# Message passing over sorted edges: the one-hots of the overflow rows computed ten gathers sooner, their products placed three gathers later, and edge numbers fetched in runs of 512 bytes

## The chip, the cores and the metric

The kernel runs on one core of one Trainium2 chip. The time is that of one execution on the device in microseconds (us); lower is better. Five engines matter: PE (TensorE) multiplies matrices, DVE (VectorE), ACT (ScalarE) and POOL (GpSimd) work on tiles in the on-chip memory, and SP issues direct transfers. Here POOL issues the indirect gathers, one instruction each. Every engine takes its instructions in the order of the program and waits at the first one that isn't ready.

## What is computed

There are N = 6250 nodes with C = 256 values and E = 100000 edges, sorted by destination. After a layer norm and a relu come four rounds of message passing, each followed by three dense layers; the input is added at the end.

```python
def agg(h):
    return jax.ops.segment_sum(h[src], dst, num_segments=N)
for l in range(NL - 1):                       # NL = 4
    h = x + agg(x)
    h = jax.nn.relu(h @ W1s[l] + b1s[l])
    h = jax.nn.relu(h @ W2s[l] + b2s[l])
    x = h @ W3s[l] + b3s[l]
h = x + agg(x)
h = jax.nn.relu(h @ cW1 + cb1)
h = jax.nn.relu(h @ cW2 + cb2)
return h @ cW3 + cb3
...
h = jnp.maximum(_layernorm(x, axis=-1), 0.0)
x = x + _L0_gnn_ref(h, src, dst, ...)
```

## The kernel before

**Nodes, blocks, panels.** The nodes stand in NT = 49 blocks of P = 128. The features, already multiplied by the next W1, lie in `XY`, each value split in a high and a low part. The sum over neighbours is made in two ways.

- *By products.* Eight panels of four blocks (`panels`) have a matrix of edge counts, one byte per entry. `build` makes it once, while layer 0 runs: for two steps of 128 edges it forms one-hots of the edges' ends on DVE (`one_hot`, L1067, tiles `lo` and `hi`, one batch ahead, two buffers each), multiplies them on PE (L1108, tile `bp`, two buffers) and casts the result to bytes (L1116 on ACT, every fourth on DVE at L1118). `product` then runs over the 49 source blocks, one *unit* each: four matmuls of 512 columns (L1566) that read one cast tile `a`. `prepare` asks for those casts (L1539 on ACT, L1541 on DVE) three units ahead in layer 0 and five later.
- *By gathers.* The blocks of `gone` (17, in layer 0 four more) get their neighbours' rows from a table in HBM. A node has K = 17 direct rows; what is beyond that goes to OV = 2 *overflow* gathers of 128 rows for the whole block, which a matmul with a one-hot of the receiving nodes distributes. So a block takes SLOT = 19 gathers (L1391, tiles `rows` and `last`).

**Order.** The program is written out unit by unit. `tick` counts units (`now`), and `later(n, f)` runs f n ticks on. `clock` adds up a planner's estimate of the PE time issued so far. The class `Gathered` spreads a layer's gathers evenly over that clock (`begin`, `pace`), and its `events` say after which gather of a block something is done: `pair` adds two tiles of rows into `acc` (L1417, L1419); `fold`, after gather 17, makes u from `XY`, `acc` and the last row (L1429 to L1437) and then the one-hot `hot` (L1439); `add`, after gather 19, multiplies the overflow rows by `hot` on PE (L1445, tile `sums`, two matmuls of which each shows as two in the profile). `finish` adds `sums` to u (L1455) and, some ticks on, transposes u on PE (L1466) and hands it to the dense layers (`mlp`, L1260 and L1289). Other bursts of matmuls are put where `meets` is true, which is when an `add` is due. In the last eight ticks of a layer all its events are due.

**Before the first unit.** `look` finds the edges' place by node, `normed` normalises and multiplies by W1. At its end `look` asks for the first K edges of every node of the 21 gathered blocks: 21 gathers of 17 numbers per partition from `src` straight into `idx` (L820, issued at L607 by `ask`). Then come PRE = 36 ticks that only build, two steps each. At the 25th, `slot_rows` turns `idx` into row numbers with two DVE instructions over all 21 blocks (L852, L853), and layer 0's gathers begin (READY = 50 steps). `overflow` computes the places of a block's overflow edges (L858 to L871) and three ticks later fetches their sources, one number per partition, two gathers, straight into `over`. It is called for the first two blocks at the 23rd and 24th tick, and for each next one while the gathers of the second block ahead of it run.

Of the kernel before, what the change touches and what calls it, by code (L numbers as in the profile page):

```python
# [8 lines left out]
F32 = mybir.dt.float32  # L9
I32 = mybir.dt.int32  # L10
# [4 lines left out]
OP = mybir.AluOpType  # L15
PSUM = bass.MemoryType.PSUM
DRAM = bass.MemoryType.DRAM
P = 128
# [378 lines left out]
def sorted_edges(  # L397
# [38 lines left out]
    nc = tc.nc  # L436
    N, C = x.shape
# [16 lines left out]
    K, OV = 17, 2  # L454
    SLOT = K + OV
# [14 lines left out]
    NG = sum(n for _, n in gone)  # L470
# [17 lines left out]
    nodes3 = const.tile([P, 3, NG], F32, name="nodes3")  # L488
    gained = const.tile([P, NG], F32, name="gained")
    from_i = over[:, 0, :]  # L490
    taken = const.tile([P, NG, 2], BF16, name="taken")
    slots = const.tile([P, OV * P], BF16, name="slots")
    kth = const.tile([P, K], F32, name="kth")
    line = const.tile([P, OV], F32, name="line")
    pad = const.tile([P, 2], F32, name="pad")
# [115 lines left out]
            after(got, "edges are asked for a few at a time")  # L611

    def look(pool):
        firsts_i = pool.tile([1, EB], I32, name="near_i", bufs=1)
        with nc.allow_non_contiguous_dma(reason="each tile's first destination"):
            nc.sync.dma_start(out=firsts_i, in_=bass.AP(tensor=dst.tensor, offset=dst.offset,
# [230 lines left out]
        yield  # L847


    def slot_rows():  # L850

        nc.vector.scalar_tensor_tensor(live, idx, pad[:, 1:2], live, op0=OP.add, op1=OP.mult)  # L852
        nc.vector.tensor_scalar(idx, live, pad[:, 0:1], None, op0=OP.add)  # L853

    def overflow(hots, c):

        hit = hots.tile([P, OV * P], BF16, name="hit", bufs=2)
        nc.vector.tensor_scalar(hit, slots, gained[:, c:c + 1], None, op0=OP.is_ge)  # L858
        ps = ps_g.tile([P, W], F32, name="pt")
        for j in range(OV):  # L860
            nc.tensor.matmul(ps[:, 2 * j:2 * j + 2], hit[:, j * P:(j + 1) * P], taken[:, c, :],
                             start=True, stop=True)
        v = ps[:, :2 * OV].rearrange("p (j t) -> p j t", t=2)
        e = hots.tile([P, OV], F32, name="e_f", bufs=2)
        e_i = hots.tile([P, OV], I32, name="e_i", bufs=2)

        def edges():
            nc.vector.tensor_copy(rel[:, c, :], v[:, :, 0])
            nc.vector.scalar_tensor_tensor(e, v[:, :, 1], nodes3[:, 2, c:c + 1], line, op0=OP.add,
                                           op1=OP.add)  # L870
            nc.vector.tensor_scalar(e_i, e, float(E - 1), None, op0=OP.min)  # L871
# [125 lines left out]
    with tc.manual_schedule():  # L997
# [160 lines left out]
        def later(n, fn):  # L1158
            due.append((now[0] + n, fn))
# [181 lines left out]
        class Gathered:  # L1341
            def __init__(self, l):
                self.l, self.sent, self.done = l, 0, 0
                self.first, self.turn = None, None
                self.blocks = [(b, n, i, left[q] + i)
                               for q, (b, n) in enumerate(gone) for i in range(n)
                               if l == 0 or (b, n) != panels[-1]]
                self.alone = {b + i for b, n, i, _ in self.blocks}
                self.rows, self.us, self.acc, self.hot = {}, [], None, None
                self.order = [(g, k) for g in range(len(self.blocks)) for k in range(SLOT)]  # L1350
                self.events = []
                for g in range(len(self.blocks)):
                    for k in range(3, K - 1, 2):
                        self.events.append((SLOT * g + k, lambda g=g, k=k: self.pair(g, k)))
                    self.events.append((SLOT * g + K - 1, lambda g=g: self.fold(g)))
                    self.events.append((SLOT * g + SLOT - 1, lambda g=g: self.add(g)))
                self.n = len(self.events)

            def due(self, early=0.0):
# [5 lines left out]
                        self.first + self.events[self.done][0] * self.pace - early))  # L1365

            def meets(self):
                return self.due() and self.events[self.done][0] % SLOT == SLOT - 1

            def begin(self):  # L1370
                self.first = clock[0] + LEADS[self.l]
# [28 lines left out]
            def advance(self):  # L1400

                if self.first is None:
                    return
                while ahead:
                    overflow(hots, ahead.pop(0))
                self.flow()
                while self.due():
                    at, run = self.events[self.done]
# [12 lines left out]
            def fold(self, g):  # L1421
                if self.turn in jobs:
                    jobs.remove(self.turn)
                    self.turn[2]()
                b, n, i, c = self.blocks[g]
                b += i
                u = work.tile([P, C], F32, name="u", bufs=2)
                self.us.append(u)
                nc.vector.tensor_tensor(u, XY[:, b, :C].bitcast(F32), XY[:, b, C:].bitcast(F32),  # L1429
                                        OP.add)  # L1430
                used.add((self.l, b, 0))
                if (self.l, b, 1) in used:
# [3 lines left out]
                nc.vector.tensor_tensor(u, u, self.acc[:, 1, :], OP.add)  # L1436
                nc.vector.tensor_tensor(u, u, self.rows.pop((g, K - 1)), OP.add)  # L1437
                self.hot = work.tile([P, OV, P], F32, name="hot", bufs=2)
                nc.vector.tensor_tensor(self.hot, colf[:, None, :].to_broadcast([P, OV, P]),  # L1439
                                        rel[:, c, :, None].to_broadcast([P, OV, P]), OP.is_equal)  # L1440

            def add(self, g):
                b, n, i, _ = self.blocks[g]
                for j in range(OV):
                    mm = nc.tensor.matmul(sums[:, :C], self.hot[:, j, :], self.rows.pop((g, K + j)),  # L1445
                                          start=(j == 0), stop=(j == OV - 1))
                    passed(C * FULL32, mm)
                self.finish(b, n, i, sums)
# [253 lines left out]
```

## Time and profile before

| what | value |
|---|---|
| median of 3 runs | 2399.58 us (2398.6 to 2402.63) |
| the profiled execution | 2401.84 us, of which its span is 2400.0 us |
| busy share of the span | PE 88%, PE weight loads 66%, POOL 63%, DVE 52%, ACT 40% |
| first unit of layer 0 | at about 186 us; layers 0 to 3 end at about 858, 1374, 1882 and 2400 us |
| DMA | 375.68 MB, mean 157 GB/s |

A row of the groups view reads: line, engine, operation, what it writes and reads, shape, count | busy us in total, mean ns of one | idle time of the engine just before these instructions, and what ended most of it. A row of the timeline: start and length in us, engine, line, operation, tiles, how many merged, and in brackets the idle time before the first and what ended it. A row of the windows view: the window, its length, busy us and instruction count of PE, PE weight loads, DVE, ACT and POOL, then the granted PE clock, the DMA share and GB/s.

### The profile page before, as it was taken

The numbers are of one execution on the slowest core, as the hardware profiler recorded it, in microseconds if no ns is written. First come the engines' busy times: TensorE is split into PE (matmuls) and PEld (weight loads), VectorE is DVE, ScalarE is ACT, GpSimd is POOL, SyncE is SP. The second block draws the span as 40 slices with busy tenths as digits, with TensorE's granted clock in tenths as the row PEclk, the third lists the DMA queues.
The fourth block names the chain that finished last, engine by engine and source line by source line (L and its number), as shares of the span: only waits on it lengthen the run. The fifth ranks groups of instructions, "written<-read, shape, count | busy, mean of one in ns | idle before, by whom it ended". The sixth has DMA issues, their size and how long they took to land.

```text
span 2400.0 us, 28926 instructions
## 1 busy us (share of the span) xinstructions
PE 2107.7 (88%) x9071; PEld 1578.9 (66%) x9071; DVE 1242.1 (52%) x2785; ACT 962.7 (40%) x1925; POOL 1515.7 (63%) x1495
## 2 busy tenths in 40 slices
PE   5858788787888899999999899989998998999898
PEld 3635565555555577777777777767776776676665
DVE  6867665655566634444344544443445444544444
ACT  4756555555455643233223342322323422232222
POOL 3346677666776627776677357776777276777773
PEclk9958999898999999999999999999999999999999
DMA  5425545544454645445455465454546454555553
GB/s 174 133 85 161 167 149 163 163 149 143 147 168 152 210 146 169 145 140 169 138 163 164 151 191 153 138 168 136 171 138 194 150 180 141 175 161 181 162 180 94
DMA packets 198743, 375.68 MB, mean 157 GB/s; under 512 B 34210, under 2 KB 125474, under 8 KB 198580
## 3 DMA queue, kind: packets, MB, share of 16 engines
q0 software_dynamic: 69024, 182.29, 25.8%
q1 hardware_dynamic: 127630, 189.61, 24.4%
q10 hardware_dynamic: 1926, 1.85, 0.3%
q8 instruction: 73, 1.20, 0.2%
q14 instruction: 90, 0.74, 0.1%
HBM read 313.88 MB, written 59.39 MB: 156 GB/s over the span
## 4 chain that ended last, share of the span: by engine, by line
PE 80%; issue 7%; DVE 5%; ACT 3%; another core or an unknown queue 3%; DMA 1%; POOL 0%; ACTq 0%; DVEq 0%; POOLq 0%
PE agg L1566 57%; PE ps L1260 6%; PE ps L1289 5%; PE bp L1108 4%; PE sums L1445 3%; ACT at L1116 1%; PE ps L1286 1%; ACT a L1539 1%; PE bp L953 1%; PE ps L1466 1%; DVE acc L1419 1%; PE ps L582 1%; DVE hi L1067 0%; DVE lo L1067 0%
## 5 line engine op out<-in xcount | busy, mean ns | idle before, releaser
L1566 PE MATMUL agg<-a,XY 128*128 128x512 f32 x6076 | 1584.7, 413 | 58.1 <-issue 34.9
L1391 POOL DMA_INDIRECT rows<-table,idx x1152 | 1179.3, 1024 | 631.0 <-PE agg L1566 245.2
L1566 PEld LDWEIGHTS agg<-a,XY 128*128 128x128 f32 x6076 | 1157.2, 195 | 340.4 <-issue 68.8
L1539 ACT CAST a<-at 128x512 fp32r<-128x512 uint8 x943 | 565.0, 623 | 797.8 <-PE agg L1566 574.2
L1541 DVE CAST a<-at 128x512 fp32r<-128x512 uint8 x576 | 257.1, 452 | 534.7 <-PE agg L1566 368.9
L1116 ACT CAST at<-bp 128x392 uint8<-128x392 f32 x402 | 184.2, 488 | 296.7 <-PE bp L1108 107.3
L1419 DVE TENSOR_TENSOR acc<-acc,rows 128x512 f32<-128x512 f32 x432 | 295.6, 684 | 2.7 <-DMA rows<-table,idx 0.4
L1108 PE MATMUL bp<-hi,lo 128*128 128x196 bf16 x1024 | 158.1, 272 | 119.1 <-issue 68.7
L1108 PEld LDWEIGHTS <-lo 128*128 128x128 bf16 x1024 | 87.3, 104 | 207.6 <-issue 154.8
L1391 POOL DMA_INDIRECT last<-table,over x144 | 154.2, 1071 | 67.4 <-PE agg L1566 27.8
L1260 PE MATMUL ps<-h,w 128*128 128x512 f32 (+2 forms) x364 | 159.3, 578 | 7.0 <-issue 7.0
L1067 DVE TENSOR_TENSOR lo<-lanes,pairs 128x512 bf16<-128x512 bf16 x256 | 107.2, 419 | 73.1 <-remote 32.1
L1067 DVE TENSOR_TENSOR hi<-cols,pairs 128x784 bf16<-128x784 bf16 x256 | 142.8, 558 | 0.0
L1289 PE MATMUL ps<-w,h 128*128 128x256 f32 x588 | 135.9, 383 | 3.5 <-ACT h L1473 1.8
L1289 PEld LDWEIGHTS ps<-w,h 128*128 128x128 f32 x588 | 112.5, 192 | 21.8 <-ACT h L1473 2.6
L1118 DVE CAST at<-bp 128x392 uint8<-128x392 f32 x110 | 62.0, 564 | 121.9 <-PE bp L1108 53.2
L1260 PEld LDWEIGHTS ps<-h,w 128*128 128x128 f32 (+1 forms) x364 | 64.8, 186 | 75.2 <-issue 69.3
L1307 DVE TENSOR_TENSOR zz<-ps,w 128x512 f32<-128x512 f32 (+1 forms) x75 | 49.8, 677 | 122.7 <-PE ps L1289 55.9
L1445 PE MATMUL sums<-last,hot 128*128 128x256 f32 x288 | 81.5, 407 | 35.7 <-DVE hot L1439 20.7
L1455 DVE TENSOR_TENSOR u<-u,sums 128x256 f32<-128x256 f32 x72 | 30.0, 417 | 139.9 <-PE agg L1566 112.7
L1445 PEld LDWEIGHTS sums<-last,hot 128*128 128x128 f32 x288 | 54.9, 198 | 63.3 <-DVE hot L1439 25.3
L1391 POOL DMA_INDIRECT last<-table,idx x72 | 75.0, 1041 | 33.5 <-issue 13.7
(167 smaller groups left out, 1080.8 us busy)
## 6 DMA issues: line engine op xcount, KB each, us to landing
at<-mat SPq DMA_DIRECT2D x214, 448.0 KB
mat<-at SPq DMA_DIRECT2D x32, 784.0 KB
rows<-table,idx POOLq DMA_INDIRECT x1152
table<-zz SPq DMA_DIRECT2D x72, 256.0 KB
back<-table SPq DMA_DIRECT2D x120, 128.0 KB
xs<-in_x_dram SPq DMA_DIRECT2D x8, 768.0 KB
table<-zs SPq DMA_DIRECT2D x24, 256.0 KB
out_dram<-zz SPq DMA_DIRECT2D x24, 256.0 KB
```

The lines of the kernel that those rows point to most:

```text
L1067: nc.vector.tensor_tensor(o.rearrange("p q (n t) -> p q n t", t=2), values.rearrange("p (n t) -> p n t", t=2)[:, None, :, :].to_broadcast( ...
L1108: mm = nc.tensor.matmul(bp[:, m * HW:(m + 1) * HW], lo[:, q + m, :], hi[:, q + m, :], start=True, stop=True)
L1116: nc.scalar.copy(o, v)
L1118: nc.vector.tensor_copy(o, v)
L1260: mm = nc.tensor.matmul(ps[:mp, :w], weights[l][0][:, c, i * P:i * P + mp], h1[:, c, :w], start=(c == 0), stop=(c == KC - 1))
L1289: mm = nc.tensor.matmul(o, h2[0][:, c, nodes], w3[:, c, :], start=(c == 0), stop=(c == KC - 1))
L1391: got = nc.gpsimd.indirect_dma_start(out=t, out_offset=None, in_=tables[self.l][:, :], in_offset=bass.IndirectOffsetOnAxis(ap=at, axis=0),)
L1419: nc.vector.tensor_tensor(self.acc, self.acc, t, OP.add)
L1445: mm = nc.tensor.matmul(sums[:, :C], self.hot[:, j, :], self.rows.pop((g, K + j)), start=(j == 0), stop=(j == OV - 1))
L1539: nc.scalar.copy(o, mat[l, p][j])
L1541: nc.vector.tensor_copy(o, mat[l, p][j])
L1566: mm = nc.tensor.matmul(agg[c][:, :w], XY[:, j, o:o + P], a[:, :w], start=(j == 0 and half == 0), stop=(j == NT - 1 and half == 1))
```

## The change

The one-hot of the overflow rows leaves `fold` and becomes an event of its own (`spots`), due after the ninth gather of its block. `add` is due three gathers later, so it falls among the next block's first gathers, but for a layer's last block. A copy of `src`, padded by 128 numbers, is written to HBM at the very start by two transfers on ACT's queue. The direct edges of a block are then fetched from it 128 numbers (512 bytes) per partition into a scratch tile of the pool `rows`, one block per tick from the first tick on, and turned into row numbers five ticks later by two small DVE instructions per block. The overflow sources are fetched 512 bytes wide too, into two scratch tiles (`run`, two buffers), and their first number is copied out six ticks after the fetch (`keep`), 42 small DVE copies in all. Layer 0's gathers begin two ticks later (READY = 54).

```diff
+    srcs = dram.tile([E + P], I32, name="srcs")
...
     def look(pool):
+        nc.scalar.dma_start(out=srcs[:E].rearrange("(p e) -> p e", p=P - 28),
+                            in_=src.rearrange("(p e) -> p e", p=P - 28))
+        nc.scalar.dma_start(out=srcs[E:].rearrange("(o e) -> o e", o=1),
+                            in_=src[:P].rearrange("(o e) -> o e", o=1))
...
-        nc.vector.tensor_scalar(at0, st, float(E - K), None, op0=OP.min)
+        nc.vector.tensor_scalar(at0, st, float(E), None, op0=OP.min)
         nc.vector.tensor_copy(from_i, at0)
-        for c in range(NG):
-            asks.append((idx[:, c, :], src, from_i[:, c:c + 1]))
-        ask(len(asks))
...
-    def slot_rows():
-        nc.vector.scalar_tensor_tensor(live, idx, pad[:, 1:2], live, op0=OP.add, op1=OP.mult)
-        nc.vector.tensor_scalar(idx, live, pad[:, 0:1], None, op0=OP.add)
+    def slot_rows(gath, c):
+        t = gath.tile([P, 2, C], F32, name="rows", bufs=7)[:, 0, :P].bitcast(I32)
+        asks.append((t, srcs, from_i[:, c:c + 1]))
+        ask(1)
+
+        def turn():
+            w = live[:, c, :]
+            nc.vector.scalar_tensor_tensor(w, t[:, :K], pad[:, 1:2], w, op0=OP.add, op1=OP.mult)
+            nc.vector.tensor_scalar(idx[:, c, :], w, pad[:, 0:1], None, op0=OP.add)
+
+        later(5, turn)
...
         def gather():
+            ts = [hots.tile([P, P], I32, name="run", bufs=2) for _ in range(OV)]
             for j in range(OV):
-                asks.append((over[:, j, c:c + 1], src, e_i[:, j:j + 1]))
+                asks.append((ts[j], srcs, e_i[:, j:j + 1]))
             ask(OV)
+
+            def keep():
+                for j in range(OV):
+                    nc.vector.tensor_copy(over[:, j, c:c + 1], ts[j][:, 0:1])
+
+            later(6, keep)
...
                 for g in range(len(self.blocks)):
+                    behind = 3 if g < len(self.blocks) - 1 else 0
+                    self.events.append((SLOT * g + 8, lambda g=g: self.spots(g), False))
...
-                    self.events.append((SLOT * g + SLOT - 1, lambda g=g: self.add(g)))
+                    self.events.append((SLOT * g + SLOT - 1 + behind, lambda g=g: self.add(g), True))
+                self.events.sort(key=lambda o: o[0])
...
+            def spots(self, g):
+                c = self.blocks[g][3]
+                hot = self.hot[g] = work.tile([P, OV, P], F32, name="hot", bufs=2)
+                nc.vector.tensor_tensor(hot, colf[:, None, :].to_broadcast([P, OV, P]),
+                                        rel[:, c, :, None].to_broadcast([P, OV, P]), OP.is_equal)
...
-                self.hot = work.tile([P, OV, P], F32, name="hot", bufs=2)
-                nc.vector.tensor_tensor(self.hot, colf[:, None, :].to_broadcast([P, OV, P]),
-                                        rel[:, c, :, None].to_broadcast([P, OV, P]), OP.is_equal)
             def add(self, g):
...
-            READY = 50
+            READY = 54
...
                 if built[0] == READY:
-                    slot_rows()
                     layers[0].begin()
+                if built[0] % 2 == 0 and built[0] // 2 <= NG:
+                    slot_rows(gath, built[0] // 2 - 1)
```

More of the change, by code (lines that the diff above doesn't have):

```diff
@@ L1348, in __init__ @@
                 self.alone = {b + i for b, n, i, _ in self.blocks}
-                self.rows, self.us, self.acc, self.hot = {}, [], None, None
+                self.rows, self.us, self.acc, self.hot = {}, [], None, {}
                 self.order = [(g, k) for g in range(len(self.blocks)) for k in range(SLOT)]
@@ L1352, in __init__ @@
                 for g in range(len(self.blocks)):
+                    behind = 3 if g < len(self.blocks) - 1 else 0
+                    self.events.append((SLOT * g + 8, lambda g=g: self.spots(g), False))
                     for k in range(3, K - 1, 2):
-                        self.events.append((SLOT * g + k, lambda g=g, k=k: self.pair(g, k)))
-                    self.events.append((SLOT * g + K - 1, lambda g=g: self.fold(g)))
-                    self.events.append((SLOT * g + SLOT - 1, lambda g=g: self.add(g)))
+                        self.events.append((SLOT * g + k, lambda g=g, k=k: self.pair(g, k), False))
+                    self.events.append((SLOT * g + K - 1, lambda g=g: self.fold(g), False))
+                    self.events.append((SLOT * g + SLOT - 1 + behind, lambda g=g: self.add(g), True))
+                self.events.sort(key=lambda o: o[0])
                 self.n = len(self.events)
@@ L1367, in meets @@
             def meets(self):
-                return self.due() and self.events[self.done][0] % SLOT == SLOT - 1
+                return self.due() and self.events[self.done][2]
             def begin(self):
@@ L1407, in advance @@
                 while self.due():
-                    at, run = self.events[self.done]
+                    at, run, _ = self.events[self.done]
                     self.send(at + 1)
@@ L1437, in fold @@
                 nc.vector.tensor_tensor(u, u, self.rows.pop((g, K - 1)), OP.add)
-                self.hot = work.tile([P, OV, P], F32, name="hot", bufs=2)
-                nc.vector.tensor_tensor(self.hot, colf[:, None, :].to_broadcast([P, OV, P]),
-                                        rel[:, c, :, None].to_broadcast([P, OV, P]), OP.is_equal)
             def add(self, g):
                 b, n, i, _ = self.blocks[g]
+                hot = self.hot.pop(g)
                 for j in range(OV):
-                    mm = nc.tensor.matmul(sums[:, :C], self.hot[:, j, :], self.rows.pop((g, K + j)),
+                    mm = nc.tensor.matmul(sums[:, :C], hot[:, j, :], self.rows.pop((g, K + j)),
                                           start=(j == 0), stop=(j == OV - 1))
```

## The prediction

> **What bounds the kernel now.** I read the page first (busy shares and the chain that ended last), then the windows by stage, then the groups around the products of the overflow rows, and last the timeline at their waits.
>
> ```profile
> PE 2107.7 (88%) x9071; PEld 1578.9 (66%) x9071; DVE 1242.1 (52%) x2785; ACT 962.7 (40%) x1925; POOL 1515.7 (63%) x1495
> PE 80%; issue 7%; DVE 5%; ACT 3%; another core or an unknown queue 3%; DMA 1%; POOL 0%; ACTq 0%; DVEq 0%; POOLq 0%
> ```
> ```profile
> 129.00:186.00 57.00, 32.08 (x151) 16.77 (x152) 36.50 (x91) 34.09 (x83) 22.84 (x23) 0.51 0.33 101
> 186.00:858.00 672.00, 556.98 (x2680) 399.07 (x2679) 417.83 (x967) 368.72 (x807) 448.80 (x433) 0.93 0.51 157
> 858.00:1374.00 516.00, 483.02 (x1977) 375.41 (x1978) 228.80 (x489) 168.42 (x310) 330.19 (x323) 0.97 0.52 158
> ```
> PE carries 80% of the chain. In layer 1 (the third window) it is busy 483 of 516 us at a granted clock of 0.97, DVE only 229; in the stage that only builds (the first window) it is busy 32 of 57 us at 0.51. So what counts is where PE stands idle. The groups of the product of the overflow rows, for the whole span, for layer 0, and for layers 1 to 3, with the units' products and the one-hot:
>
> ```profile
> L1445 PE MATMUL sums<-last,hot 128*128 128x256 f32 x288 | 81.5, 407 | 35.7 <-DVE hot L1439 20.7 <-issue 5.5 <-DVE u L1436 5.3
> L1445 PE MATMUL sums<-last,hot 128*128 128x256 f32 x84 | 23.3, 401 | 5.9 <-DVE hot L1439 5.8
> L1445 PE MATMUL sums<-last,hot 128*128 128x256 f32 x204 | 58.1, 410 | 29.8 <-DVE hot L1439 15.0 <-issue 5.5 <-DVE u L1436 5.3
> L1566 PE MATMUL agg<-a,XY 128*128 128x512 f32 x4704 | 1174.2, 406 | 51.8 <-issue 32.0 <-DVE a L1541 8.4 <-ACT a L1539 8.2
> L1439 DVE TENSOR_TENSOR hot<-colf,rel 128x256 f32<-128x256 f32 x72 | 30.1, 419 | 0.0
> ```
> PE is idle for 35.7 us before 288 of its 9071 matmuls, and most of that ends with the one-hot. Its 72 instructions cost DVE only 0.42 us each, but `fold` puts each behind the four additions that make u, so whenever DVE is late the product, due two gathers on, finds no one-hot. The six longest waits, and the product without one:
>
> ```profile
> 838.51 2.30 PE L1445 MATMUL sums<-last,hot 128*128 128x256 f32 x4 [3.72 <-DVE hot L1439]
> 1087.79 1.13 PE L1445 MATMUL sums<-last,hot 128*128 128x256 f32 x4 [3.50 <-DVE u L1436]
> 1336.65 2.08 PE L1445 MATMUL sums<-last,hot 128*128 128x256 f32 x4 [6.74 <-DVE hot L1439]
> 1598.03 2.08 PE L1445 MATMUL sums<-last,hot 128*128 128x256 f32 x4 [3.73 <-DVE hot L1439]
> 1681.69 2.08 PE L1445 MATMUL sums<-last,hot 128*128 128x256 f32 x4 [5.50 <-issue]
> 1846.01 1.13 PE L1445 MATMUL sums<-last,hot 128*128 128x256 f32 x4 [3.18 <-DVE u L1437]
> 414.52 1.03 PE L1445 MATMUL sums<-last,hot 128*128 128x256 f32 x4
> ```
> These six are 26.4 of the 35.7 us.
>
> **The change part by part.** The sum is made against the profiled execution, 2401.84 us; its span is 2400.0. The median of the three runs, 2399.58, lies 2.3 below it, and that is taken off at the end.
>
> *(a) The one-hot sooner, the product later.* The product then needs the one-hot, ten to thirteen gathers old, and the last rows, asked for before `fold`. Nothing it reads is late any more, so its 35.7 us go as such. What is late next are the casts `a` that the next units read. The longest wait shows how many stand ready:
>
> ```profile
> 1324.98 4.94 PE L1566 MATMUL agg<-a,XY 128*128 128x512 f32 x20
> 1326.00 0.43 DVE L1541 CAST a<-at 128x512 fp32r<-128x512 uint8 x1 [2.32 <-PE agg L1566]
> 1327.49 0.62 ACT L1539 CAST a<-at 128x512 fp32r<-128x512 uint8 x1 [3.07 <-PE agg L1566]
> 1334.76 0.62 ACT L1539 CAST a<-at 128x512 fp32r<-128x512 uint8 x1 [6.65 <-remote]
> ```
> PE went through five units in 4.94 us, 0.99 us each, while two casts were made. Six units can be ready at most (its own and five ahead), so 6 - 5 + 2 = 3 were left, 3.0 us of work; the next cast came at 1334.76. I cap each of the six long waits at 3.0: 18.0, and take the other 35.7 - 26.4 = 9.3 whole. Gain 27; at most 35.7, at least the 9.3.
>
> *(b) The clock.* After waits of 3.7 us and more the four matmuls take 2.08 us or more instead of 1.03; after 3.50 and 3.18 only 1.13. Four such waits give 4 x 1.05 = 4 us, from the product alone. The Trainium skill, page "TensorE: Matmul & The Clock Gate" (Part 1), says that an idle window of about 3.4 us halves PE's clock until a busy window of the same length has passed; as an estimate from it, each of the four costs half of 3.4 us, 7 us in all, and the sum below would be 3 us lower. The rows agree on where the step lies. I keep 4; between 0 and 8.
>
> *(c) The stage that builds.* Now 21 gathers are issued one per tick, each followed five ticks later by two DVE instructions on 128x17. None such is in the trace. Nearest are the pair on 128x2 in `overflow`; above them the pair on 128x357 that goes:
>
> ```profile
> L869 DVE SCALAR_TENSOR_TENSOR e_f<-pt,nodes,line 128x2 f32<-128x2 f32 x21 | 4.4, 208 | 0.0
> L871 DVE TENSOR_SCALAR e_i<-e_f 128x2 int32<-128x2 f32 x21 | 3.9, 184 | 0.7
> L852 DVE SCALAR_TENSOR_TENSOR live<-idx,pad,live 128x357 f32<-128x357 int32 x1 | 0.6, 586 | 0.0
> L853 DVE TENSOR_SCALAR idx<-live,pad 128x357 int32<-128x357 f32 x1 | 0.4, 408 | 0.0
> ```
> ```profile
> 133.00:150.00 17.00, 4.18 (x18) 1.92 (x17) 3.60 (x8) 4.03 (x9) 11.28 (x12) 0.50 0.07 7
> 151.00:168.00 17.00, 13.27 (x61) 6.80 (x60) 13.92 (x34) 13.68 (x34) 0.00 (x0) 0.50 0.28 94
> ```
> A tick has four of these matmuls, so the smooth stretch from 151 on makes 61/4 = 15.2 ticks in 17 us, 1.11 us each, with DVE idle (17 - 13.92)/15.2 = 0.20 us of each. A pair costs 0.39; 0.19 shows, 21 times, 4.0 us; the two that go give back 1.0. Cost +3, between -1 and +7.
>
> Will the pair wait for its fetch, with the one-hots `lo` and `hi` queued behind it and PE behind those? The trace holds gathers of just such runs (`wd`, `ws`: 128 numbers per partition):
>
> ```profile
> 49.87 1.33 POOL L607 DMA_INDIRECT ws<-in_src_dram,starts  x1 [0.30 <-issue]
> 51.51 0.97 POOL L607 DMA_INDIRECT wd<-in_dst_dram,starts  x1 [0.31 <-issue]
> 52.90 0.43 DVE L743 TENSOR_SCALAR hi<-ws 98x512 int32<-98x512 int32 x1 [2.45 <-DMA ws<-in_src_dram,starts]
> ```
> Landing is 52.90 - 51.20 = 1.7 us after the issue ends, and POOL needs 0.97 + 0.30 = 1.27 us per gather. Asked at a tick, used 5 x 1.11 = 5.6 us on: 2.6 us to spare, of which POOL loses 1.27 - 1.11 = 0.16 per tick, 3.4 over 21; DVE's own added time slows the ticks by as much. At most the last few wait, under 1 us; I put nothing.
>
> *(d) The padded copy.* It moves 0.4 MB, read and written, on the queue ahead of the first weights. The first 40 us run at this rate:
>
> ```profile
> 0.00:40.00 40.00, 16.94 (x50) 11.32 (x50) 28.26 (x66) 14.99 (x29) 9.40 (x31) 0.96 0.60 182
> ```
> 0.8 MB at 182 GB/s is 4.4 us if everything stood behind it; the DMA share is 0.60, so 0 if it fits between. I take +1.
>
> *(e) Overflow sources.* The two copies wait for their fetch six ticks after asking, with one-hots and additions behind them. In layer 0:
>
> ```profile
> 186.00:858.00 672.00, 410.10 (x1372) 258.40 (x1371) 0.93 0.51 157
> L607 POOL DMA_INDIRECT over<-in_src_dram,e_i x38 | 39.4, 1038 | 11.6 <-issue 9.8 <-DVE hi L1067 0.6 <-PE bp L1108 0.6
> L868 DVE COPY rel<-pt 128x2 f32<-128x2 f32 x19 | 2.9, 153 | 12.4 <-PE pt L861 7.3 <-issue 3.0 <-PE bp L1108 1.5
> ```
> 1372/4 = 343 units in 672 us: 1.96 us a tick, so 11.8 us of cover against 2 x 1.34 + 1.7 = 4.4 for two gathers. Six more rows queued on POOL would still fit. The 42 copies are 42 x 0.153 = 6.4 us of a DVE that is idle for 254 us of the layer: 0, and 6.4 with the cover gone. Without those six ticks a part of the 21 fetches would be met in flight. The second block's scratch tiles come free only with the first one's copies, five ticks on, so POOL stands about 5.5 us with the first rows of layer 0 behind it; those are asked for 13 planner microseconds ahead: 0.
>
> *(f) Begin two ticks later.* 2.2 us; POOL's 433 instructions at 1.27 need 550 of layer 0's 672 us, and the pace is drawn up anew to the same end: 0. In the other layers nothing is moved past a layer's end, since the last block's product keeps its place.
>
> Sum: -27 - 4 + 3 + 1 = -27. 2401.84 - 27 = 2374.8, less 2.3: **2373 us** as the median.
>
> **The rivals.**
>
> *R1, slower: the stop only moves to the casts.* At 1334.76 the cast on ACT is released in the same microsecond as DVE's work, after 6.65 us. If PE's lead over DVE and ACT is used up at each product, whatever it stops at, the idle time before L1566 grows by what L1445 loses. Then (a) and (b) are nothing and the costs stand: up to +7 from (c), +4.4 from (d): 2399.6 + 11.4 = 2411. The Trainium skill, same page, section on architectural detail, has DVE and ACT strictly first in, first out: by it whatever is late on DVE delays all behind it, the pairs of (c) and the casts alike. Against R1: three units stood ready even at the longest wait, and casts end only 8.4 + 8.2 us of idle time in three layers. It decides if that sum grows by over 25 us.
>
> *R2, faster still: the slow stretch goes with the short runs.* From 133 to 150 us the build stage makes 18 matmuls where 151 to 168 makes 61; POOL issues the 17-number gathers until just before. If they are the cause, and wide ones don't slow it, (61 - 18)/61 x 17 = 12 us go: 2361. Page "DMA: Bandwidth & Descriptors" of the Trainium skill (Specifications) gives 512 bytes as the least for full rate, with a read-modify-write below. Against it:
>
> ```profile
> L607 POOL DMA_INDIRECT idx<-in_src_dram,over x21 | 21.2, 1011 | 39.2 <-PE ps L829 33.1 <-issue 6.1
> q0 software_dynamic: 69024, 182.29, 25.8%
> q0 software_dynamic: 672, 0.18, 6.5%
> ```
> Over the span a packet of this queue takes 0.258 x 16 x 2400 / 69024 = 0.144 us; in the window 120 to 150 us, which holds the 21 short gathers, 0.065 x 16 x 30 / 672 = 0.046. The DMA share there is 0.07: the engines are not what is slow.
>
> *R3, no change: the long waits give nothing back.* DVE and ACT are let go together, by something with its own time; what PE does meanwhile is lost at the next such stop. The nine short waits remain: -9.3 + 4 = -5, 2394; with a little more cost, no difference.
>
> **How the numbers follow.** Forecast 0.61, R1 0.17, R2 0.12, R3 0.10. The forecast's own range is 2360 (all of (a), the upper (b), -35.7 - 8 + 4) to 2389 (18 from (a), with (c) and (d) at their upper bounds, -18 - 4 + 11.4). For 8 in 10 I reach down to 2355, which holds R2 and half of what (a) and (b) may bring beyond the sum (2361 - 12.7/2), and up to 2405, which holds R3 and R1 at half its costs. A measurement of this kernel can tell about 0.2%, 4.8 us. Faster: 0.61 + 0.12 = 0.73; same: 0.10; slower: 0.17.
>
> **What would show it.** Idle before L1445 falls from 35.7 to under 5 us, with none of it ended by `hot`; idle before L1566 in layers 1 to 3 grows from 51.8 by less than 15; the stage from 129 to 186 us is 2 to 4 us longer, with DVE nearer to full; layers 1 and 2, which hold five of the six long waits, shorten by some 10 us each, layer 3 hardly. I am wrong if L1566 takes over the waits (R1), if the `keep` copies show idle time ended by their DMA, or if layer 0 gets longer.

## The result, and the profile after

The changed kernel takes 2417.59 us (median of five runs, 2413.65 to 2422.26) beside 2399.58 us for the kernel before (five runs, 2391.3 to 2402.63). The ratio is 1.0071, 95% interval 1.0050 to 1.0093: slower by some 18 us, where a gain of 27 us was forecast. The profiled run after took 2413.65 us (span 2411.8), that of before 2401.84, so the two traces account for 11.8 of the 18 us.

The page after, busy times; then the windows that the prediction showed of before (PE, PEld, DVE, ACT, POOL busy, granted clock, DMA share, GB/s); then the groups of the product in the whole span and in layers 1 to 3, of the units' products in layers 1 to 3, and of the one-hot:

```profile
PE 2112.3 (88%) x9071; PEld 1573.5 (65%) x9071; DVE 1248.5 (52%) x2867; ACT 961.9 (40%) x1925; POOL 1515.5 (63%) x1495
```
```profile
129.00:186.00 57.00, 31.84 (x150) 15.79 (x150) 42.89 (x134) 34.36 (x83) 28.02 (x28) 0.52 0.43 129
186.00:858.00 672.00, 557.34 (x2658) 401.69 (x2659) 419.80 (x1006) 368.55 (x806) 451.55 (x434) 0.92 0.53 161
858.00:1374.00 516.00, 481.06 (x1976) 367.71 (x1975) 226.85 (x486) 166.90 (x307) 331.31 (x323) 0.99 0.52 157
```
```profile
L1468 PE MATMUL sums<-last,hot 128*128 128x256 f32 x288 | 78.5, 393 | 8.7 <-DMA last<-table,over 5.2 <-issue 3.5
L1468 PE MATMUL sums<-last,hot 128*128 128x256 f32 x204 | 55.3, 390 | 5.6 <-issue 3.5 <-DMA last<-table,over 2.1
L1589 PE MATMUL agg<-a,XY 128*128 128x512 f32 x4704 | 1173.3, 405 | 77.7 <-issue 31.6 <-ACT a L1562 24.7 <-DVE a L1564 6.8
L1444 DVE TENSOR_TENSOR hot<-colf,rel 128x256 f32<-128x256 f32 x72 | 30.0, 417 | 0.0
```

The product's idle time fell from 35.7 to 8.7 us, none of it ended by `hot`, as forecast. But in layers 1 to 3 it fell by 24.2 us (29.8 to 5.6), and the idle time before the units' products there grew by 25.9 (51.8 to 77.7). So the wait went from the product to the units, and no time came of it there. The windows show that the build stage made as many matmuls as before (150, before 151), with 6.4 us more work on DVE, and that layer 0 is 22 matmuls behind at 858 us.

From first unit to first unit, layer 0 takes 678.0 us (before 673.1), layers 1 and 2 take 513.8 and 513.2 (before 515.4 and 508.5), and layer 3 to the end 520.6 (before 517.4). Layers 1 and 2 together are 3 us longer, where they were to be some 20 shorter. Layer 0 got longer, which the prediction had named as a sign of being wrong. PE's idle time in it is the same (115.5 us, before 115.6); it is PE's busy time that grew, from 557.4 to 562.5, at a granted clock of 0.92 after 0.93. One trace of each kernel can't tell whether a few us in a layer come from the change.

Two new stops are seen in the trace after. The first, on its timeline at the end of the build stage (start, duration, and in brackets the idle time before and what ended it):

```profile
176.07 0.20 DVE L891 COPY over<-run 128x1 int32<-128x1 int32 x2
176.95 0.96 POOL L608 DMA_INDIRECT run<-srcs,e_i  x1 [3.86 <-PE bp L1125]
178.21 0.95 POOL L608 DMA_INDIRECT run<-srcs,e_i  x1 [0.30 <-issue]
181.42 0.15 DVE L891 COPY over<-run 128x1 int32<-128x1 int32 x1 [4.33 <-DMA run<-srcs,e_i]
183.20 0.15 DVE L891 COPY over<-run 128x1 int32<-128x1 int32 x1 [1.63 <-DMA run<-srcs,e_i]
184.29 0.83 PE L1125 MATMUL bp<-hi,lo 128*128 128x196 bf16 x4 [6.13 <-DVE hi L1084]
```

POOL may issue the second block's two fetches only when the first block's copies, at 176.07, have freed the scratch tiles (the row names PE as the releaser; e7 below shows that it is the tiles). The second block's own copies come due one tick after the first's, find nothing landed, and DVE stands 4.33 + 1.63 us with the one-hots `hi` and `lo` behind it; PE stands 6.13.

The second, at the end of layer 3, PE's timeline of before and then of after:

```profile
2373.13 1.93 PE L1260 MATMUL ps<-h,w 128*64 128x512 f32 x4
2374.99 1.13 PE L1445 MATMUL sums<-last,hot 128*128 128x256 f32 x4
```
```profile
2383.28 1.03 PE L1468 MATMUL sums<-last,hot 128*128 128x256 f32 x4
2386.28 1.93 PE L1277 MATMUL ps<-h,w 128*64 128x512 f32 x4
2398.59 0.62 PE L1277 MATMUL ps<-h,w 128*64 128x128 f32 x4 [1.60 <-DVE zz L1318]
```

The work that hangs on the last but one product (`ps<-h,w`) stood ahead of the last product and now stands behind it. From the last product to the end of the span are 25.0 us before (2374.99 to 2400.0) and 28.5 after (2383.28 to 2411.8).

### The profile page after: what moved, and what is told of

It reads as the page before. It is cut to its first block, busy times and chain, and to the rows that moved or that the text cites. A ratio compares the mean times of both kernels' runs of the same rounds, so it can differ in the third digit from the quotient of the medians.

```text
span 2411.8 us, 28894 instructions
## 1 busy us (share of the span) xinstructions
PE 2112.3 (88%) x9071; PEld 1573.5 (65%) x9071; DVE 1248.5 (52%) x2867; ACT 961.9 (40%) x1925; POOL 1515.5 (63%) x1495
## 5 line engine op out<-in xcount | busy, mean ns | idle before, releaser
L1280 ACT ACTIVATE h<-ps,bias 128x512 f32<-128x512 f32 (+2 forms) x91 | 58.4, 663 | 107.7 <-PE agg L1589 47.2
L1468 PE MATMUL sums<-last,hot 128*128 128x256 f32 x288 | 78.5, 393 | 8.7 <-DMA last<-table,over 5.2
```

What stands on the lines that cost most here:

```text
L1468: mm = nc.tensor.matmul(sums[:, :C], hot[:, j, :], self.rows.pop((g, K + j)), start=(j == 0), stop=(j == OV - 1))
```

## The experiments

The 16 changed kernels were each timed against the kernel before on the same chip. On the four chips that they ran on, the kernel before takes 2188.89 to 2194.34 us (medians of five groups) and not 2399.58; so the ratios below are compared with each other, and what they say of the pair above is argued from its traces.

### e1, e2, e3, e4: the parts

The one-hot alone sooner (e1), the product alone later (e2), both (e3), and the fetch part alone (e4); only the lines that matter are shown:

```diff
 e1  +self.events.append((SLOT * g + 8, lambda g=g: self.spots(g), False))      # hot leaves fold
 e2  +behind = 3 if g < len(self.blocks) - 1 else 0                              # hot stays in fold
     +self.events.append((SLOT * g + SLOT - 1 + behind, lambda g=g: self.add(g), True))
 e3  both;   e4  srcs, slot_rows per block, run/keep, READY = 54; events as before
```

> The kernel before, with the one-hot alone ten gathers sooner; the product of the overflow rows stays two gathers behind the fold, nothing is fetched wide. Theory S (the stop only moves: what PE gains at the product it loses at the casts, and the change's cost lies in the wide fetch): idle before the product falls from 35.7 us to under 15, idle before the units' matmuls grows by as much, time within 5 us of 2400. Theory L (the later product is what costs): time as before or up to 15 us less, 2385 to 2400. My forecast's step (a): about 15 us less, since the one-hot ends 20.7 of the 35.7 us.

> The kernel before, with the product alone three gathers later; the one-hot stays in the fold. Theory S: within 5 us of 2400, idle time moved from the product to the units. Theory L: the later product also delays u + sums, the turns and the planner's match of jobs with products, so 10 to 20 us slower, 2410 to 2420, most of it in layers 0 and 3. Step (a) of the forecast: 20 us less.

> The kernel before, with both moves (one-hot sooner, product three gathers later), nothing fetched wide. Theory S: 2395 to 2405. Theory L: 2408 to 2420, as the whole change. Step (a) of the forecast with fetch costs far above its sum: 2370 to 2380.

> The kernel before, with the fetch part alone (padded copy, edge runs and overflow sources 512 bytes wide, layer 0 begins two ticks later), one-hot and product where they were. Theory S: 2410 to 2420, as the whole change. Theory L: 2395 to 2405. The forecast's steps (c) to (f): 2404; with step (a) right and the whole change 18 us slower, they would have to cost some 45: 2440.

Measured: e1 1.0000 (0.9986 to 1.0014), e2 1.0084 (1.0055 to 1.0113), e3 1.0064 (1.0046 to 1.0082), e4 1.0071 (1.0057 to 1.0085). Theory S falls for e2 and e3, Theory L for e4: both halves cost. Step (a) had given e1 about 15 us; it gives none. Why is read from the product's group, first in the kernel before on these chips (b0, next), then in e1:

```profile
L1445 PE MATMUL sums<-last,hot 128*128 128x256 f32 x288 | 80.8, 400 | 40.8 <-DVE hot L1439 27.5 <-DMA last<-table,over 13.3
```
```profile
L1451 PE MATMUL sums<-last,hot 128*128 128x256 f32 x288 | 81.2, 398 | 35.2 <-DMA last<-table,over 29.0 <-DVE u L1443 6.0
```

With the one-hot out of the way, and the product in its old place, the product waits almost as long, now for the fetch of the overflow rows.

### b0 and f0: the two kernels on these chips

b0 is the kernel before unchanged, f0 the whole change.

> The kernel before, unchanged, for its trace beside the others: the experiments' chip runs it in 2193 us where the profile of before took 2401.84. If that chip lacks the episodes in which TensorE's signals reach DVE and ACT late, the build stage takes 43 us without the slow stretch of 18 matmuls in 17 us, so the short fetches were not its cause (R2's mechanism falls), and the product's idle time is ended by its fetch, not by the one-hot. If the short fetches are the cause, the stretch is there again.

> The whole change, for its parts' sum: the moves alone took 1.0064 of the time before and the fetch alone 1.0071. If the two costs lie in different places (the fetch in the build stage and layer 0, the moves at the ends of layers 0 and 3), they add to 1.0135: 2222 us where before takes 2193. If both delay the same end of layer 0 and overlap there, 1.007 to 1.009: 2209 to 2213.

Measured: b0 2190.55 us in one run; f0 1.0155 (1.0126 to 1.0184), 2228.47 us. Within the intervals the parts add: 0.0064 + 0.0071 = 0.0135. The page of b0 and the first 17 us of its build stage:

```profile
PE 2031.4 (93%) x9071; PEld 1546.1 (71%) x9071; DVE 1243.8 (57%) x2785; ACT 970.2 (44%) x1925; POOL 1521.0 (69%) x1495
```
```profile
129.00:146.00 17.00, 13.56 (x64) 7.30 (x63) 14.23 (x34) 13.60 (x34) 13.34 (x13) 0.50 0.33 93
```

64 matmuls in 17 us, with the short fetches running: they alone do not make the slow stretch of the profile of before (18 in 17 us). On these chips R2's mechanism falls. The build stage takes 42.8 us, as expected of b0; that the product's idle time would be ended by its fetch was not met, since the one-hot ends 27.5 of the 40.8 us.

### e5 and e6: the two halves of the fetch

Each with the padded copy; e5 the edge runs wide, e6 the overflow sources wide.

> The kernel before with the padded copy and the edge runs alone fetched wide, 21 gathers and 21 pairs of DVE instructions in the build stage; the overflow sources are fetched as before. Theory K (most of the fetch part's cost is the copies that keep the overflow sources, which stop DVE until their fetch lands): only the pairs (21 x 0.2 = 4 us) and the copy (2.5 us) are left, 1.003, 2200 us where before takes 2193. Theory P (the 21 pairs and their gathers cost it): 1.007, 2208.

> The kernel before with the padded copy and the overflow sources alone fetched wide; the edge runs are fetched as before. Theory K: the second block's fetches wait for the first block's scratch tiles, its copies stop DVE some 6 us in the build stage, and part of the 50 us of DVE idle time before these copies in layer 0 reaches PE: 1.004 to 1.006, 2202 to 2206 us where before takes 2193. Theory P: the copy alone shows, 1.001, 2196.

Measured: e5 1.0017 (0.9999 to 1.0035), e6 1.0048 (1.0029 to 1.0068), as Theory K has it. In the trace of e4, which has both, a tick of the build stage reads:

```profile
152.47 0.56 DVE L1084 TENSOR_TENSOR hi<-cols,pairs 128x784 bf16<-128x784 bf16 x1
152.95 0.23 DVE L860 SCALAR_TENSOR_TENSOR live<-rows,pad,live 128x17 f32<-128x17 int32 x1
153.09 0.83 PE L1125 MATMUL bp<-hi,lo 128*128 128x196 bf16 x4 [0.39 <-DVE hi L1084]
153.22 0.24 DVE L861 TENSOR_SCALAR idx<-live,pad 128x17 int32<-128x17 f32 x1
154.31 0.83 PE L1125 MATMUL bp<-hi,lo 128*128 128x196 bf16 x4 [0.39 <-DVE hi L1084]
```

DVE is full and a tick takes 1.22 us. Without the pair it takes 17 x 4 / 64 = 1.06 (the window of b0). Times 21 that is a little over 3 us, and in all 21 pairs the fetch was waited for under 1 us.

### e7: another place for the second block's fetches

```diff
-            ts = [hots.tile([P, P], I32, name="run", bufs=2) for _ in range(OV)]
+            if c == layers[0].blocks[1][3]:
+                two = gath.tile([P, 2, C], F32, name="rows", bufs=7)
+                ts = [two[:, j, :P].bitcast(I32) for j in range(OV)]
+            else:
+                ts = [hots.tile([P, P], I32, name="run", bufs=2) for _ in range(OV)]
```

> The fetch part alone again, but the second block's two overflow fetches land in a free tile of the ring of gathered rows, so that they need not wait for the first block's copies; all else as in the fetch part alone, which took 1.0071 of the time before. Theory K (the wait for scratch tiles stops POOL 3.9 us and then, through the copies that DVE stands at, 6 us more, and all of it ends in layer 0's gathers): DVE stands under 1 us at these copies in the build stage, the gathers of layer 0 end 8 to 10 us sooner, 1.003, 2200 us where before takes 2194. Rival: only the copies' idle time goes and layer 0 ends where it did, 1.007, 2209.

Measured: 1.0047 (1.0030 to 1.0064) against e4's 1.0071. The stop is gone; the timeline of e7 at the place shown above:

```profile
168.46 0.96 POOL L608 DMA_INDIRECT rows<-srcs,e_i  x1 [0.30 <-PE bp L1129]
173.16 0.15 DVE L895 COPY over<-rows 128x1 int32<-128x1 int32 x1 [0.94 <-DMA rows<-srcs,e_i]
```

The second block's first copy starts at 172.08, one tick after the first block's, and before its second DVE stands 0.94 us. POOL had issued the last gather of layer 0 by 770.9 us, in e4 by 781.9. The ratios differ by 0.0024, 5 us, with intervals that overlap a little: the scratch tiles are one cause, smaller than Theory K had it, and its size is rough.

### e8: the last two products in place

```diff
-                    behind = 3 if g < len(self.blocks) - 1 else 0
+                    behind = 3 if g < len(self.blocks) - 2 else 0
```

> Both moves without the wide fetch, as before 1.0064 of the time before, but the product of the last two blocks of each layer keeps its place, not of the last alone. Theory E (the cost of the later product lies at the ends of the layers, where the last but one product comes three gathers later and what hangs on it falls behind the last product): layer 3 takes 472 us as before, not 478, and the time is 0.999 to 1.001, 2192 to 2196. Rival (every later product costs): 1.005 to 1.006, 2206.

Measured: 0.9987 (0.9973 to 1.0000) against e3's 1.0064. PE's timeline at the end of layer 3, first of e3, then of e8:

```profile
2169.73 1.22 PE L1452 MATMUL sums<-last,hot 128*128 128x256 f32 x2 [4.99 <-DMA last<-table,over]
2171.77 1.22 PE L1452 MATMUL sums<-last,hot 128*128 128x256 f32 x2 [0.82 <-DMA last<-table,over]
2176.76 2.40 PE L1260 MATMUL ps<-h,w 128*64 128x512 f32 x4
```
```profile
2152.07 1.93 PE L1260 MATMUL ps<-h,w 128*64 128x512 f32 x4
2157.59 0.70 PE L1452 MATMUL sums<-last,hot 128*128 128x256 f32 x2 [1.56 <-DMA last<-table,over]
2159.67 0.70 PE L1452 MATMUL sums<-last,hot 128*128 128x256 f32 x2 [1.38 <-DMA last<-table,over]
```

In e3 PE has nothing left to do while the last rows are fetched, stands 4.99 us, and does the work of the last but one block afterwards: 32.6 us from the last product to the end (span 2204.4), in e8 24.7 (span 2184.4). From first unit to first unit, layers 1, 2 and 3 (to the end) take 469.9, 470.7 and 478.1 us in e3, 465.7, 463.8 and 468.9 in e8; layer 0 takes the same in both. Theory E holds: the cost of the moves is that one product, the last but one, of each later layer. The other traces bear this out for layers 2 and 3. The 14 kernels that keep these products in place take 462.8 to 464.9 us for layer 2 and 468.9 to 475.4 for layer 3; the three that don't (e2, e3, f0) take 466.0 to 470.7 and 478.1 to 481.2. Layer 1 can't be told apart: it takes 465.3 to 473.1 us with them in place.

Away from the ends the moves together bring 0.13%, at the edge of what can be told from nothing. Where the product's wait went is seen in PE's groups, in b0 (the product's own row stands above, with 40.8 us idle), then in e8:

```profile
L1566 PE MATMUL agg<-a,XY 128*128 128x512 f32 x6076 | 1526.7, 404 | 5.2 <-ACT h L1582 2.2 <-ACT a L1539 2.1 <-DVE a L1541 0.9
L1108 PE MATMUL bp<-hi,lo 128*128 128x196 bf16 x1024 | 151.8, 269 | 51.1 <-DVE hi L1067 39.8 <-ACT at L1116 5.5 <-DVE at L1118 2.7
```
```profile
L1573 PE MATMUL agg<-a,XY 128*128 128x512 f32 x6076 | 1528.2, 404 | 14.1 <-DVE a L1548 9.3 <-ACT h L1589 2.8 <-ACT a L1546 2.1
L1108 PE MATMUL bp<-hi,lo 128*128 128x196 bf16 x1024 | 153.0, 270 | 66.0 <-DVE hi L1067 50.9 <-DVE at L1118 6.2 <-ACT at L1116 5.4
L1452 PE MATMUL sums<-last,hot 128*128 128x256 f32 x288 | 77.7, 389 | 15.0 <-DMA last<-table,over 15.0
```

Before the product 25.8 us of idle time went; 8.9 came back before the units and 14.9 before the build products, most of it ended by what DVE makes next, the casts `a` and the one-hots `hi`.

### e9 and e10: when layer 0's gathers begin

```diff
-            READY = 50
+            READY = 66     # e9;  42 in e10
```

> The kernel before with one number changed: layer 0's gathers begin 8 ticks of the build stage later. Theory G (on this chip POOL issues the gathers of layer 0 back to back, and the layer ends some 22 us after the last of them): 8 ticks of 1.06 us, 8.5 us, come out at the end: 1.0039, 2203 us where before takes 2194. Step (f) of the forecast (the pace is drawn up anew to the same end): no difference.

> The kernel before with the same number changed the other way: layer 0's gathers begin 4 ticks sooner. Theory G: 4 x 1.06 = 4.2 us less, 0.998, 2190 us where before takes 2194, unless PE's own work then bounds the layer. Step (f) of the forecast: no difference. It is also the change that these runs point to for a version faster than both.

Measured: e9 1.0005 (0.9987 to 1.0023), e10 0.9962 (0.9948 to 0.9976). The first and the last gather of layer 0 and the first unit of layer 1, in e10, then in e9:

```profile
156.78 1.10 POOL L1391 DMA_INDIRECT rows<-table,idx  x1 [0.30 <-DVE hi L1067]
759.59 0.96 POOL L1391 DMA_INDIRECT last<-table,over  x1 [0.30 <-issue]
782.23 1.19 PE L1566 MATMUL agg<-a,XY 128*128 128x512 f32 x4 [1.11 <-ACT a L1539]
```
```profile
169.71 1.09 POOL L1391 DMA_INDIRECT rows<-table,idx  x1 [0.30 <-DVE hi L1067]
765.95 0.96 POOL L1391 DMA_INDIRECT last<-table,over  x1 [0.30 <-issue]
789.80 1.20 PE L1566 MATMUL agg<-a,XY 128*128 128x512 f32 x4 [1.12 <-ACT a L1539]
```

In both, layer 1 begins 21.7 to 22.9 us after POOL has issued the last gather. But a begin 12.9 us later ends only 6.4 us later, and in e9 eight ticks show no cost against the kernel before. Theory G holds sooner and fails later. In e9 POOL makes up for the late begin early in the layer: from 172 to 200 us it is busy 21.9 us, in b0, which had begun at 160.87, only 18.7. The gain of e10, 8 us, is twice what Theory G had. Its trace shows half: layer 1 begins at 782.23 us and in b0 at 786.59. The number of the change, two ticks later, is not its cost.

### e13 and e14: what is left of the fetch

e13 makes the padded copy and never reads it. e14 is e6 with e7's place for the second block, and the copies later:

```diff
-            later(6, keep)
+            later(12, keep)
```

> The kernel before with the padded copy made and never read. Step (d) of the forecast: +1 us, between 0 and 4.4: 1.000 to 1.002. If the copy is what is left of the fetch part's cost, 1.002 to 1.003, with the prelude 4 to 6 us longer.

> The overflow sources alone fetched wide (1.0048), with the second block's fetches in the ring of rows and the copies 12 ticks after the asking, not 6. If DVE's standing at these copies in layer 0 costs what is left: its idle time there falls from 52 us to under 15, and the time to 1.000 to 1.001, 2194. If DVE only stands there instead of at the gathered rows, which come late anyway: the idle time moves back to the additions of the rows and the time is 1.002 to 1.003, 2199, as with the scratch tiles repaired alone.

Measured: e13 1.0010 (0.9994 to 1.0027), e14 1.0013 (0.9998 to 1.0027). The copies and the additions of the rows on DVE and the build products on PE in layer 0 (us busy, mean ns, idle time before), in e6, then in e14:

```profile
L886 DVE COPY over<-run 128x1 int32<-128x1 int32 x38 | 5.5, 151 | 60.1 <-DMA run<-srcs,e_i 59.8
L1431 DVE TENSOR_TENSOR acc<-acc,rows 128x512 f32<-128x512 f32 x126 | 86.4, 686 | 23.2 <-DMA rows<-table,idx 22.7
L1120 PE MATMUL bp<-hi,lo 128*128 128x196 bf16 x887 | 121.8, 255 | 59.8 <-DVE hi L1079 55.0 <-DVE at L1130 1.5 <-ACT at L1128 0.2
```
```profile
L890 DVE COPY over<-run 128x1 int32<-128x1 int32 x38 | 4.0, 143 | 0.8 <-DMA run<-srcs,e_i 0.8
L1435 DVE TENSOR_TENSOR acc<-acc,rows 128x512 f32<-128x512 f32 x126 | 86.7, 688 | 88.1 <-DMA rows<-table,idx 84.8 <-issue 2.5 <-DVE at L1134 0.5
L1124 PE MATMUL bp<-hi,lo 128*128 128x196 bf16 x876 | 119.6, 255 | 37.2 <-DVE hi L1083 29.8 <-DVE over L890 3.5 <-DVE at L1134 1.5
```

Neither expectation is met as a whole: DVE's idle time went back to the additions, as in the second, and yet nearly all the cost went, as in the first. PE's idle time before the build products fell by 22.6 us, but that before its other products in layer 0 grew, the overflow rows' from 14.8 to 22.2 and that of the overflow places (`pt`) from 3.2 to 16.5, and the layer's idle time as a whole fell by under 4 us. The build stage is shorter, 46.6 us in e6 and 42.8 in e14 as in b0, but layer 0 then takes 621.2 us in e14 after 616.1, so that layer 1 begins only 1.5 us sooner (792.1, in e6 793.6). e14 also has e7's place for the second block. So these two runs show that the two repairs together take the cost away, and not the way by which the copies' wait reaches the end.

### e12, e15 and e11: the repairs together

e12 is the whole change with the repairs of e7 and e8, e15 that with the copies after 12 ticks; e11 is e8 with READY = 42.

> The whole change with both repairs: the last two products of a layer in place, and the second block's overflow fetches into a free tile of the ring of rows. If these two causes explain the change's cost, what is left is the fetch part's 1.0047 less the 0.0013 that the moves bring: 1.003 to 1.004, 2201 us where before takes 2193 and the whole change 2228. If they don't: 1.008 or more, 2211.

> The whole change with both repairs of e12 and the copies of the overflow sources 12 ticks after asking, not 6. If the copies' stop in layer 0 is what e12 leaves (1.0066), only the 21 pairs (4 us), the padded copy (2 us) and the moves' 0.0013 gain are left: 1.001 to 1.003, 2192 to 2197 us where before takes 2190, and PE's idle time before the build products in layer 0 falls from 66 us to under 55. If another cause is hidden: 1.005 or more, 2201.

> The kernel before with both moves, the last two products of a layer kept in place (alone 0.9987), and layer 0's gathers begun 4 ticks sooner (alone 0.9962), nothing fetched wide. If the two add: 0.995, 2182 us where before takes 2193. If both gain at the same end of layer 0: 0.996 to 0.997, 2185.

Measured: e12 1.0066 (1.0045 to 1.0088), between its two expectations, e15 1.0032 (1.0017 to 1.0048), just above the lower one, e11 0.9965 (0.9953 to 0.9978). So three repairs take 1.0155 to 1.0032, and that interval just takes in e5's 1.0017, the pairs with the copy. From e12 to e15 only the copies' place differs: 0.0034. Layer 0 takes 620.7 us in e12 and 615.8 in e15, and PE's idle time before the build products in it falls from 66.0 to 52.6, as expected. e11 is faster than both kernels, but no faster than e10 alone: nearly all of it is the earlier begin.

## Why the prediction was wrong, step by step

*(a) -27, the step that failed.* What failed is the step from idle time to time: six long waits at 3.0 us each, and the nine short ones whole, were counted as gained. The wait itself went. "Nothing it reads is late any more" held nearly in the given pair, where 8.7 us are left (with both moves on the experiments' chips 24.2 in e3 and 15.0 in e8, all of it for the overflow rows). But PE stood again at the next thing that DVE or ACT had to make. In the given pair 24.2 us went in layers 1 to 3 and 25.9 came before the units; in e8, the best case of the moves, 25.8 went and 23.8 came, and the gain is 0.0013, some 3 us. The three units at the longest stop were worked out from the most that can be ready, and said nothing of the next stop; nothing in the trace showed that the lead would be rebuilt in between. That is R1, which I gave 0.17, and its 2411 is the nearest of the four sums. Its own threshold was put two ways: the idle time before the units' products grew by 25.9, the part of it ended by casts only from 16.6 to 31.5. So its mechanism is borne out with a wider list of late things than the casts.

*(b) -4.* The product's matmuls did get shorter, 81.5 to 78.5 us, near the 4. PE's busy time as a whole grew by 4.6 (by 5.1 in layer 0, in the other layers some up and some down), so the gain was lost elsewhere.

*(c) +3 and (d) +1.* Right: e5 has 1.0017, 3.7 us, with the copy in it, and e13 1.0010, 2 us, neither told from zero. Of the pairs in e4 one waited for its fetch, 0.83 us.

*(e) 0, failed.* The prediction named the wait of POOL for the second block's scratch tiles and set it at 0, because the rows behind it had time. It did not follow the clock of `keep`, which runs from the asking and not from the issue: DVE meets the late fetch and stops. On the chips of the experiments the scratch tiles cost 0.0024 (e4 to e7) and the early copies another 0.0034 (e12 to e15). Of the second cost the given pair shows little: DVE stands 66.9 us at these copies in the trace of f0, but 6.8 in the trace after, 6.0 of them in the stop shown above. The cover of "11.8 us against 4.4" left out that POOL's queue itself may be behind. The Trainium skill, page "TensorE: Matmul & The Clock Gate" (section on architectural detail), has DVE strictly first in, first out; the trace agrees, with the two copies of 0.15 us each that held PE for 6.13 us.

*(f) 0.* Right for the size in question (e9), for a reason other than the one given: the end is not fixed. e9 and e10 differ by 6.4 us in their last gather, and e10 shows that a sooner begin comes out sooner.

*The term that was missing.* "In the other layers nothing is moved past a layer's end, since the last block's product keeps its place" looked at one product only. The last but one, three gathers later, cost 0.0077 of the time, from e3 to e8: the largest single cost. In the given pair it is seen as 3.5 us at the end of layer 3; its share in the other layers there was not separated (layers 1 to 3 take 1547.5 us after, 1541.3 before).

*R2 and R3.* R2's slow stretch is absent from the trace after (47 matmuls from 133 to 150 us, where before had 18), but b0 shows the short fetches without it. A page of the Trainium skill that the prediction weighed, "DMA: Bandwidth & Descriptors" (Specifications), gives 512 bytes as the least for full rate; no run here gains by the width. R3's long waits that give nothing back are what happened to (a), but with costs beside it. One reading that R1 and R3 share was off: in the trace of before DVE had been at work from 1333.19 us on, and what was released with ACT's cast at 1334.76 was a gather of POOL, at 1334.84.

*What stays open.* In the given pair the change costs 0.71%, on the experiments' chips 1.55%. The pair's trace shows the stop of 6.13 us and the 3.5 us at the end, and a build stage of the same length only because the slow stretch stood in before's. Of the 4.9 us in layer 0, with PE's idle time unchanged, the cause is open. Why both kernels run some 9% slower there, and whether the stretch would be there in another run, no experiment could tell.

## What to carry to other kernels

When a wait is taken away, look up what else the waiting instruction reads and when that lands, and then what the same late engine makes for the instructions behind it: the idle time is gained only if those are ready too, at this stop and at the next. A step moved later by a few places must be followed at the last places of every loop, the last but one too, where no work is left to cover it. And a consumer timed from the asking of a transfer needs cover for the whole queue before the issue, not for the transfer alone.

## What the runs showed of the hardware

The same kernel takes 2189 to 2194 us (medians) on four chips and 2400 in the given pair, whose chip is not on record. The matmul count is the same; PE's busy time is 2031.4 (b0) against 2107.7 us, and the rest of the span, in which PE does not work, 157 against 292 us. What differs beside it is how soon ACT follows PE. Where ACT had stood idle before a cast of a build product in layer 0, the cast began 0.04 us after the last build matmul's end in all 156 cases of b0; in the trace of before 41% of 175 began more than 0.35 us after it, the latest 9.0 us. The cause isn't shown.

POOL issues a gather of 128 rows each 1.25 us or more, about 0.95 us of it busy and 0.30 between two, for rows of 68, 512 and 1024 bytes alike: in the build stage the wide edge runs of the trace after take it

```profile
L608 POOL DMA_INDIRECT rows<-srcs,over x21 | 20.6, 982 | 52.7 <-PE bp L1125 48.4 <-issue 3.0 <-DVE live L860 1.0
```

982 ns, the short ones of before took 1011. Between issue and landing the time varies more. The data of the two fetches of the stop shown first were there 3.5 and 4.0 us after their issue ended (177.91 to 181.42, 179.16 to 183.20), twice the 1.7 us that the prediction had read off a quieter place of the trace.
